# Masking the diagonal blocks in the search for the maxima: from TensorE products to a fused VectorE operation

## The chip, the cores and the metric

The kernel runs on one core of one Trainium2 chip. The metric is the device time of one execution in microseconds; lower is better. All times here are of that core.

## The reference

Two layers, each an attention and a feed-forward, on one sequence of 2048 tokens of 256 features. Both attentions have 16 heads of 16 features and are causal. Cut to what matters (layer 1; layer 0 differs in how q, k and v come about):

```python
scores = jnp.einsum('bhqd,bhkd->bhqk', q, k) / math.sqrt(Hd)
causal = jnp.triu(jnp.full((S, S), -jnp.inf, dtype=scores.dtype), k=1)
scores = scores + causal[None, None]
attn = jax.nn.softmax(scores, axis=-1)
out = jnp.einsum('bhqk,bhkd->bhqd', attn, v)
...
x = x + _layernorm(_L1_attn_ref(_layernorm(x, axis=-1), ...), axis=-1)
x = x + _layernorm(_L1_ffn_ref(_layernorm(x, axis=-1), ...), axis=-1)
```

The softmax needs the largest unmasked score of each row, and the kernel finds it ahead of the exponentials.

## The kernel before, in words

The 2048 tokens are four chunks c of 512 (four tiles t of 128 rows). The 16 heads are four groups g of four: inside a group, e (0 or 1) says in which half of the partitions a head lies, 64 rows each, and i (0 or 1) which of two slots. A *unit* is a chunk and a group (c, g); the order of a layer's 16 units is (0,0), (0,1), the twelve of c = 1, 2, 3, and then (0,2), (0,3). An attention layer does two things for each unit:

- **The search for the maxima** (`maxima`, line 698). Scores are formed with queries on the partitions, a bank of PSUM (128 x 512) at a time, and VectorE reduces each stretch of a row to its largest (line 737), into `pm`. Keys of earlier chunks are unmasked: 16 blocks of 512 for each earlier chunk. The diagonal chunk has for each i and e the blocks "a" (tile 3, 512 keys), "b" (tile 2, 384 keys, and tile 0, 128 keys) and "c" (tile 1, 256 keys). In the last 128 keys of each the causal mask must act. TensorE adds it: two products of 64 rows in bf16 (line 728) put the mask into the bank, and the score products (line 718) of those 128 columns accumulate on top; the other columns are a product of their own. At the end VectorE takes the largest over the chunks and splits it into two parts (lines 758 to 761), and TensorE turns the result (line 770).
- **The weighted sum** (`weighted`, line 785). With keys on the partitions, TensorE forms mask-free scores minus the maximum (lines 802 and 807), ScalarE takes the exponential (line 813), GpSimd zeroes the masked part of diagonal tiles (line 817), and TensorE multiplies by the values (line 824), which accumulate in one bank over all key tiles.

A block of the search uses one half of TensorE's rows, so the blocks of e = 0 and e = 1 run at the same time. The search of unit n may begin once the first score product of unit n-2 is out, and it runs beside the weighted sum of the units before it.

The order in which instructions stand on each engine is written out by a planner (class `Plan`). Each operation is entered with an assumed duration in us, its reads and writes, and a *rank* (its wished place in units). The planner steps through an imagined time: of all operations that are ready it finds the one that could start earliest, and then takes, on that engine, the one of lowest rank among those that could start within `near` of it. `near` is 0.3 us, but 0.1 in the feed-forward stages. Eight PSUM banks are given out by class `Banks`: at most two pairs (for the scores of the weighted sum) and at most four single banks, of which the accumulating value product holds one. The planner fixes only the order; on the chip each engine runs its queue in order and waits on semaphores. Projections of the next chunk, the output projection and the layer norms are entered in the same plan.

Of the kernel before, what the change touches and what calls it, by code (L numbers as in the profile page):

```python
# [11 lines left out]
F32 = mybir.dt.float32  # L12
F32R = mybir.dt.float32r
BF16 = mybir.dt.bfloat16
# [3 lines left out]
ALU = mybir.AluOpType  # L18
AX = mybir.AxisListType
# [11 lines left out]
P = 128  # L31
CH = 512
NCHUNK = T // CH
TPC = CH // P
# [6 lines left out]
NEG = -3.0e38  # L41
# [23 lines left out]
class Buf:  # L65


    def __init__(self, make, ring=None, banks=0):
        self.make, self.ring, self.banks = make, ring, banks
        self.tile, self.at = None, ()  # L70
        self.users, self.writers, self.readers = [], [], []
        if ring is not None and banks != 1:
            ring.asked.append(self)
# [67 lines left out]
class Plan:  # L141
# [6 lines left out]
    free, mode = {}, None  # L148
    LAG = {"DVE": 0.08, "ACT": 0.1, "PE": 0.2}

    def __init__(self, near=0.3, waiting=0.1):
        self.ops, self.near, self.waiting = [], near, waiting

    def op(self, engine, us, fn, r=(), w=(), after=(), hold=(), rank=0.0, mode=None, lanes=(0, 1), lag=0.0):
# [94 lines left out]
def kernel(ctx: ExitStack, tc: tile.TileContext, x_in, cols_in, rows_in, wd_in, wuq_in, rot_in,  # L249
                         wk0_in, wv0_in, rep_in, wo0_in, wq1_in, wk1_in, wv1_in, wo1_in, ffn0_in, ffn1_in, out):  # L250
    nc = tc.nc
    PSUM = bass.MemoryType.PSUM

    const = ctx.enter_context(tc.tile_pool(name="const", bufs=1))
# [9 lines left out]
    def new(pool, shape, dtype, tag, name, n):  # L264

        ring = rings.setdefault(tag, Ring(n, True))
        assert len(ring.slots) == n
        return Buf(lambda: pool.tile(shape, dtype, tag=tag, name=name, bufs=n), ring)

    def bank(name):  # L270
        b = Buf(lambda: psum[:, b.at[0], :], banks, 1)
        return b

    def two_banks(name):
        b = Buf(lambda: psum[:, b.at[0]:b.at[0] + 2, :], banks, 2)
        return b
# [28 lines left out]
    plan = Plan()  # L305
# [8 lines left out]
    def setup(engine, us, fn, rank):  # L314

        done = Buf(lambda: None)
        plan.op(engine, us, fn, r=[late], w=[done], rank=rank)
        return done
# [90 lines left out]
    make_identity(nc, ident)  # L409


    half16 = const.tile([P, 2, P], BF16, tag="half16", name="half16")
    mask_qk = const.tile([P, 2, 2, P], BF16, tag="mask", name="mask")

    def make_mask():
        nc.gpsimd.memset(half16, 0.0)
        nc.gpsimd.memset(mask_qk, 0.0)
        for e in range(2):
            at = half16[64 * e:64 * e + 64]
            nc.gpsimd.affine_select(out=at, in_=at, compare_op=ALU.not_equal, fill=1.0, base=0,  # L420
                                    pattern=[[64, 2], [-1, P]], channel_multiplier=1)
            at = mask_qk[64 * e:64 * e + 64]
            nc.gpsimd.affine_select(out=at, in_=at, compare_op=ALU.is_ge, fill=NEG, base=0,
                                    pattern=[[64, 2], [0, 2], [-1, P]], channel_multiplier=1)

    mask_b = setup("POOL", 2.8, make_mask, rank=-3.2)


    sel_f = const.tile([P, 2, P], F32, tag="sel_f", name="sel_f")
# [233 lines left out]
    class Attention:  # L663


        def __init__(self, L, proj):
            self.L, self.proj = L, proj
            self.V = [values.tile([P, TPC, VW], F32, tag=f"V{c}", name=f"V{L}{c}") for c in range(NCHUNK)]
            self.vb = [Buf(lambda: None) for c in range(NCHUNK)]
            self.kb = [[Buf(lambda: None) for g in range(NG)] for c in range(NCHUNK)]  # L670
            self.tiles, self.k, self.q, self.loaded, self.begun, self.scores = {}, {}, {}, set(), {}, {}
            self.before = {c: [] for c in range(NCHUNK)}
# [25 lines left out]
    def maxima(layer, plan, n, qb, first_rank, span):  # L698

        (c, g), L, kb = UNITS[n], layer.L, layer.kb  # L700
        pm, mx_ = Buf(lambda: pms[n % 2], rpm), Buf(lambda: mx[n % 2], rmx)
        full = 4 * (TPC * c + 3)
        step = [0]

        def rank():
            step[0] += 1
            return first_rank + span * step[0] / full

        def block(name, i, e, terms, us, kc, reduces):


            s = bank(f"m{L}{n}{i}{name}{e}")
            b = slice(64 * e, 64 * e + 64)
            rk = rank()

            def fill():
                def part(t, k0, to, width, start, stop):
                    nc.tensor.matmul(s.t[:, to:to + width], qb.t[b, i, t * P:(t + 1) * P],  # L718
                                     layer.K(kc)[b, 2 * g + i, k0:k0 + width], start=start, stop=stop)

                if kc < c:
                    for t, k0, k1, to in terms:
                        part(t, k0, to, k1 - k0, True, True)
                    return

                lo = terms[0][3] + terms[0][2] - terms[0][1] - P
                for x in range(2):
                    nc.tensor.matmul(s.t[:, lo:lo + P * len(terms)].rearrange("p (d k) -> p d k", k=P), half16[b, x, :],  # L728
                                     mask_qk[b, x, 0:len(terms), :], start=x == 0, stop=False)
                for j, (t, k0, k1, to) in enumerate(reversed(terms)):  # L730
                    part(t, k1 - P, to + k1 - k0 - P, P, False, j == len(terms) - 1)
                part(t, k0, to, k1 - k0 - P, True, True)

            plan.op("PE", us, fill, r=[qb, kb[kc][g], mask_b], w=[s], hold=[pm],
                    after=layer.scores.get(n - 2, ()), rank=rk, mode="row", lanes=(e,))
            for red_us, t, p, src in reduces:
                plan.op("DVE", red_us, lambda t=t, p=p, src=src: nc.vector.tensor_reduce(  # L737
                    pm.t[:, t, e, i, p:p + 1], s.t[:, src], AX.X, ALU.max), r=[s], w=[pm], rank=rk)


        for i in range(2):
            for e in range(2):
                block("a", i, e, [(3, 0, CH, 0)], 0.45, c, [(0.6, 3, 0, slice(0, CH))])
            for e in range(2):
                block("b", i, e, [(2, 0, 3 * P, 0), (0, 0, P, 3 * P)], 0.8, c,
                      [(0.47, 2, 0, slice(0, 3 * P)), (0.2, 0, 0, slice(3 * P, CH))])
            for e in range(2):
                block("c", i, e, [(1, 0, 2 * P, 0)], 0.4, c, [(0.34, 1, 0, slice(0, 2 * P))])
        for i in range(2):
            for t in range(TPC):  # L750
                for p in range(c):
                    for e in range(2):
                        block(f"{t}{p}", i, e, [(t, 0, CH, 0)], 0.233, p, [(0.6, t, 1 + p, slice(0, CH))])

        def close():
            m = mx_.t
            best = small.tile([P, TPC, 2, 2], F32, tag="top", name=f"top{L}{n}", bufs=4)
            nc.vector.tensor_reduce(best, pm.t[:, :, :, :, 0:c + 1], AX.X, ALU.max)
            hl = m.rearrange("p t (e r s) -> p t e r s", e=2, s=2)
            nc.vector.tensor_scalar(hl[:, :, :, 0:2, 0].bitcast(F32R), best, -1.0, None, ALU.mult)  # L760
            nc.vector.scalar_tensor_tensor(hl[:, :, :, 0:2, 1], best, -1.0, hl[:, :, :, 0:2, 0],
                                           ALU.mult, ALU.subtract)

        rk = first_rank + span
        plan.op("DVE", 0.6, close, r=[pm, mx_b], w=[mx_], rank=rk)
        s = bank(f"mt{L}{n}")

        def flip():
            for t in range(TPC):
                nc.tensor.transpose(s.t[:, t * P:(t + 1) * P], mx_.t[:, t, :], ident)  # L770

        mrow = new(const, [P, CH], F32R, "mrow", f"mrow{L}{n}", 3)
        plan.op("PE", 0.5, flip, r=[mx_], w=[s], hold=[mrow], rank=rk, mode="full")
        plan.op("ACT", 0.50, lambda: nc.scalar.copy(mrow.t, s.t), r=[s], w=[mrow], rank=rk)
        return mrow
# [149 lines left out]
    def ffn(own, sg_at, su_at, after=()):  # L925

        L, wb = own.L, own.wb
        wg, wu, wdn = own.part(1, 0, 2), own.part(1, 1, 2), own.part(2, 0, 8)
        with tc.tile_pool(name=f"ff{L}", bufs=1) as ff:
            for tag in ("sl", "fu", "fh", "fl", "yT"):  # L930
                rings.pop(tag, None)
            plan = Plan(0.1, 0.1)

            def back(c, halves, rank):

# [30 lines left out]
            for n_, c in enumerate(own.order):  # L966
# [4 lines left out]
                for fc in range(8):  # L971
                    rk = 10 * n_ + fc
                    s = two_banks(f"gu{L}{c}{fc}")
# [67 lines left out]
    def project1(plan, c, rank):  # L1041
# [4 lines left out]
        for n in range(2) if c == 0 else ():  # L1046
            layer1.begin(plan, n, Buf(lambda n=n: ffn0.part(3, 1, 4)[:, 2 * n:2 * n + 2, :]), 43 + n, 1.0)

    ffn(ffn0, C_SG0, C_SU0, [(1, weights1), (0, lambda plan, rank: project1(plan, 0, rank)),
                             (2, lambda plan, rank: project1(plan, 1, rank))])  # L1050
    load_f8(1, ffn1_in)
    layer1.before[3] = [o for qb, _ in layer1.begun.values() for o in qb.readers]
    wo1, wo1_b = w1.tile([P, 2, D], F32, tag="wo1", name="wo1"), Buf(lambda: None)
    plan = Plan()
    plan.op("SP", 0.1, lambda: nc.sync.dma_start(out=wo1, in_=wo1_in), w=[wo1_b], rank=-5.0, lag=4.0)
    attention(layer1, plan, wo1, wo1_b, "bo1", 0.25, prepare(ffn1))
    ffn(ffn1, C_SG1, C_SU1)


# [113 lines left out]
```

## Time and profile before

| what | value |
|---|---|
| time, median of 3 runs | 1359.1 us (1357.12 to 1359.5) |
| the profiled execution: its time | 1358.62 us |
| its span, first to last instruction | 1356.9 us |
| mean granted TensorE clock | 0.964 |
| attention of layer 0, first search done to last weighted sum | 62.8 to 583.0 us |
| attention of layer 1, the same | 728.2 to 1241.5 us |
| reductions of 512, 384, 256, 128 elements: number | 896, 128, 128, 128 |
| products for the search, mask products | 1664, 768 as built |

The profile is of one execution. A row of the costliest groups names the line, the engine, the operation, what it writes and reads with shapes, the number, then busy time and the mean ns of one, then the engine's idle time before such instructions and what ended it. Busy times are unions of records[...]. The ends of TensorE's records are modelled: its busy share overstates what it does. A row of the waits names who waited for whom, the total in us, how often, and the longest.

### The profile page before, as it was taken

The page shows a single profiled execution, that of the slowest core. Times are in us where ns is not written, and L with a number is a line of the kernel's source. Part 1 is how long each engine was busy: PE and PEld are TensorE (multiplying, and loading weights), DVE is VectorE, ACT ScalarE, POOL GpSimd, SP SyncE. Part 2 cuts the span into 40 slices and gives each one's busy share as a digit, 9 for nine tenths or more (in the row PEclk, how much of TensorE's full clock was granted, in tenths as well). Part 3 has the DMA queues.
Part 4 walks back from the last instruction along what each step waited for, and adds up shares of the span by engine and source line. Part 5 has one row for each costly group of instructions (what it writes and reads, how often), then busy time and mean ns, then how long its engine had stood idle before and what let it go on. Part 6 is the DMA issues. An engine that isn't in the chain of part 4 may idle for free.

```text
span 1356.9 us, 23929 instructions
## 1 busy us (share of the span) xinstructions
PE 1268.2 (93%) x9272; PEld 749.4 (55%) x9272; DVE 932.3 (69%) x1970; ACT 797.7 (59%) x1100; POOL 291.9 (22%) x474
## 2 busy tenths in 40 slices
PE   5889999999999999989978999999999999998996
PEld 3555555555455454568756555445555545455785
DVE  3578888788988782445546868967898888345442
ACT  2336555666556768656633555565655766776563
POOL 4021101200020001346521101010000100023664
PEclk8689999999999999889989999999999999998898
DMA  5550500040000000010056050004000000000000
GB/s 162 177 165 17 172 16 17 5 153 17 17 17 17 1 16 17 25 55 1 3 169 187 1 156 21 27 5 152 17 17 17 1 17 17 17 1 1 0 32 32
DMA packets 39219, 66.29 MB, mean 49 GB/s; under 512 B 6595, under 2 KB 11040, under 8 KB 38976
## 3 DMA queue, kind: packets, MB, share of 16 engines
q1 hardware_dynamic: 38768, 64.32, 15.2%
q8 instruction: 73, 1.20, 0.4%
q0 software_dynamic: 48, 0.11, 0.1%
q10 hardware_dynamic: 288, 0.31, 0.1%
q14 instruction: 42, 0.34, 0.1%
HBM read 41.66 MB, written 23.07 MB: 48 GB/s over the span
## 4 chain that ended last, share of the span: by engine, by line
PE 74%; DVE 12%; ACT 5%; POOL 3%; DMA 3%; issue 2%; SPq 1%; POOLq 0%; ACTq 0%; DVEq 0%
PE banks L824 17%; PE banks L718 12%; PE banks L802 12%; DVE pm L737 9%; PE banks L807 9%; PE banks L588 8%; PE banks L977 7%; PE banks L943 4%; ACT pt L813 3%; PE banks L728 2%; PE banks L504 2%; DMA K<-sc_k 1%; PE banks L837 1%; PE banks L770 1%; ACT yn_a L480 1%
## 5 line engine op out<-in xcount | busy, mean ns | idle before, releaser
L737 DVE TENSOR_REDUCE pm<-banks 128x1 f32<-128x512 f32 (+3 forms) x1280 | 688.0, 603 | 169.3 <-PE banks L718 165.2
L813 ACT ACTIVATE pt<-banks 128x1024 f32<-128x1024 f32 (+3 forms) x640 | 547.2, 895 | 314.2 <-PE banks L807 297.6
L718 PE MATMUL banks<-K,Q 64*128 64x512 f32 (+3 forms) x1608 | 310.9, 383 | 12.3 <-DMA Q<-sc_q 9.0
L802 PE MATMUL banks<-mrow,sel 64*128 64x512 f32 (+3 forms) x1280 | 286.7, 413 | 18.1 <-ACT pt L813 6.3
L824 PE MATMUL banks<-pt,V 128*32 128x512 f32 (+3 forms) x2560 | 300.4, 544 | 1.2 <-ACT pt L813 0.7
L817 POOL TENSOR_SCALAR_AFFINE_SELECT pt<-pt 128x256 f32<-128x256 f32 x256 | 103.1, 406 | 751.6 <-ACT pt L813 749.5
L718 PEld LDWEIGHTS banks<-K,Q 64*128 64x128 f32 x1608 | 181.7, 192 | 124.4 <-DVE pm L737 77.5
L807 PE MATMUL banks<-Q,K 64*128 64x512 f32 (+3 forms) x1248 | 250.0, 368 | 0.0
L802 PEld LDWEIGHTS banks<-mrow,sel 64*128 64x128 f32 x1280 | 143.0, 188 | 167.6 <-ACT pt L813 98.9
L807 PEld LDWEIGHTS banks<-Q,K 64*128 64x128 f32 x1248 | 140.4, 189 | 8.5
L977 PE MATMUL banks<-F,F 128*128 128x512 f32 x512 | 132.4, 401 | 7.7 <-DVE fu L986 7.4
L977 PEld LDWEIGHTS banks<-F,F 128*128 128x128 f32 x512 | 96.8, 191 | 29.3 <-DVE fu L986 8.3
L824 PEld LDWEIGHTS banks<-pt,V 128*32 128x32 f32 x2560 | 52.5, 109 | 85.7 <-issue 69.4
L986 DVE SCALAR_TENSOR_TENSOR fu<-banks,cols,sl 128x512 f32<-128x512 f32 x64 | 47.5, 749 | 73.6 <-ACT sl L984 40.0
L989 POOL TENSOR_TENSOR fl<-fu,fh 128x512 fp32r<-128x512 f32 x64 | 81.9, 1289 | 72.8 <-ACT fh L988 72.8
L728 PE MATMUL banks<-mask,half 64*128 64x128 bf16 (+1 forms) x768 | 90.9, 247 | 1.5 <-DMA Q<-sc_q 0.7
L728 PEld LDWEIGHTS <-half 64*128 64x128 bf16 x768 | 40.8, 97 | 52.1 <-issue 49.5
L988 ACT CAST fh<-fu 128x512 fp32r<-128x512 f32 x64 | 39.6, 620 | 35.3 <-DVE fu L986 33.7
L943 PE MATMUL banks<-fl,F 128*128 128x512 f32 x128 | 51.8, 405 | 2.2 <-POOL fl L989 2.2
L943 PE MATMUL banks<-fh,F 128*128 128x512 f32 x128 | 53.0, 414 | 0.0
L984 ACT ACTIVATE sl<-banks,cols 128x512 f32<-128x512 f32 x64 | 43.3, 688 | 12.0 <-PE banks L977 11.5
L530 DVE SCALAR_TENSOR_TENSOR k<-banks,bk,k 128x512 fp32r<-128x512 f32 x16 | 12.0, 751 | 30.1 <-ACT k L528 27.4
(126 smaller groups left out, 945.9 us busy)
## 6 DMA issues: line engine op xcount, KB each, us to landing
K<-sc_k SPq DMA_DIRECT2D x128, 128.0 KB
Q<-sc_q SPq DMA_DIRECT2D x120, 128.0 KB
sc_q<-q SPq DMA_DIRECT2D x48, 256.0 KB
sc_k<-k SPq DMA_DIRECT2D x32, 256.0 KB
x<-in_x_dram SPq DMA_DIRECT2D x4, 512.0 KB
out_dram<-x SPq DMA_DIRECT2D x4, 512.0 KB
f<-in_ffn_dram SPq DMA_DIRECT2D x2, 768.0 KB
rows<-in_rows_dram SPq DMA_DIRECT2D x1, 1024.0 KB
```

The costliest lines, as they stand in the source:

```text
L588: nc.tensor.matmul(s.t[:, at:at + n], a, b, start=start, stop=stop)
L718: nc.tensor.matmul(s.t[:, to:to + width], qb.t[b, i, t * P:(t + 1) * P], layer.K(kc)[b, 2 * g + i, k0:k0 + width], start=start, stop=stop)
L728: nc.tensor.matmul(s.t[:, lo:lo + P * len(terms)].rearrange("p (d k) -> p d k", k=P), half16[b, x, :], mask_qk[b, x, 0:len(terms), :], sta ...
L737: plan.op("DVE", red_us, lambda t=t, p=p, src=src: nc.vector.tensor_reduce(pm.t[:, t, e, i, p:p + 1], s.t[:, src], AX.X, ALU.max), r=[s], ...
L802: nc.tensor.matmul(s.t[:, e, 0:nq], sel[b:b + 64, i, :], mrow.t[b:b + 64, off:CH], start=True, stop=False)
L807: nc.tensor.matmul(s.t[:, e, 0:nq], layer.K(kt // TPC)[b:b + 64, 2 * g + i, k * P:(k + 1) * P], qb.t[b:b + 64, i, off:CH], start=False, st ...
L813: plan.op("ACT", 0.1 + nq / 620, lambda s=s, pt=pt, nq=nq: nc.scalar.activation(pt.t[:, :, 0:nq], s.t[:, :, 0:nq], AF.Exp, scale=scale), r ...
L817: plan.op("POOL", 0.41, lambda pt=pt: nc.gpsimd.affine_select(out=pt.t[:, :, 0:P], in_=pt.t[:, :, 0:P], compare_op=ALU.is_ge, fill=0.0, ba ...
L824: nc.tensor.matmul(av.t[32 * j:32 * j + 32, off:CH], Vs[kt // TPC][:, kt % TPC, DV * h:DV * h + 32], pts[kt, j // 2].t[:, j % 2, 0:nq], st ...
L943: nc.tensor.matmul(dn[dh].t, wdn[:, fc, dh * P:(dh + 1) * P], halves[fc][j].t, start=fc == 0 and j == 0, stop=fc == 7 and j == 1)
L977: nc.tensor.matmul(s.t[:, i, :], w[:, cc, fc * P:(fc + 1) * P], xT[j].t[:, cc, :], start=n == 0, stop=n == 3)
L989: plan.op("POOL", 1.3, lambda fu=fu, fh=fh, fl=fl: nc.gpsimd.tensor_tensor(fl.t, fu.t, fh.t.bitcast(F32), ALU.subtract), r=[fu, fh], w=[fl ...
```

## The change

The mask leaves TensorE. A float32 tile of 128 x 512 (zero, and the mask in its last 128 columns) is made once. A diagonal block is now filled by plain score products, and VectorE's reduction of it becomes `tensor_tensor_reduce`: sum of the bank and the tail of the mask tile, and the largest of the sums, in one call. Its full-size output goes to a scratch tile `unread` (bf16), the largest to `pm`. Reductions of earlier chunks stay as they were. The two "c" blocks (i = 0 and 1) of a half now share one bank, so a unit has 10 diagonal blocks instead of 12. The assumed durations follow: a reduction of k elements, fused or not, counts 0.07 + k/965 us, a diagonal block 0.233 or 0.25 us on TensorE. The default of `near` falls from 0.3 to 0.1 us, which the feed-forward stages had already.

```diff
-    def __init__(self, near=0.3, waiting=0.1):
+    def __init__(self, near=0.1, waiting=0.1):
...
-    half16 = const.tile([P, 2, P], BF16, tag="half16", name="half16")
-    mask_qk = const.tile([P, 2, 2, P], BF16, tag="mask", name="mask")
+    mask_qk = const.tile([P, CH], F32, tag="mask", name="mask")
+    unread = const.tile([P, CH], BF16, tag="unread", name="unread")
...
-    mask_b = setup("POOL", 2.8, make_mask, rank=-3.2)
+        at = mask_qk[:, CH - P:CH]
+        nc.gpsimd.affine_select(out=at, in_=at, compare_op=ALU.is_ge, fill=NEG, base=0, pattern=[[-1, P]], channel_multiplier=1)
+
+    mask_b = setup("POOL", 1.0, make_mask, rank=-3.2)
...
-        full = 4 * (TPC * c + 3)
+        full = 4 * (TPC * c + 2) + 2
...
-                lo = terms[0][3] + terms[0][2] - terms[0][1] - P
-                for x in range(2):
-                    nc.tensor.matmul(s.t[:, lo:lo + P * len(terms)].rearrange("p (d k) -> p d k", k=P), half16[b, x, :],
-                                     mask_qk[b, x, 0:len(terms), :], start=x == 0, stop=False)
-                for j, (t, k0, k1, to) in enumerate(reversed(terms)):
-                    part(t, k1 - P, to + k1 - k0 - P, P, False, j == len(terms) - 1)
-                part(t, k0, to, k1 - k0 - P, True, True)
-
-            plan.op("PE", us, fill, r=[qb, kb[kc][g], mask_b], w=[s], hold=[pm],
-                    after=layer.scores.get(n - 2, ()), rank=rk, mode="row", lanes=(e,))
-            for red_us, t, p, src in reduces:
-                plan.op("DVE", red_us, lambda t=t, p=p, src=src: nc.vector.tensor_reduce(
-                    pm.t[:, t, e, i, p:p + 1], s.t[:, src], AX.X, ALU.max), r=[s], w=[pm], rank=rk)
+                for i, t, k, to in terms:
+                    nc.tensor.matmul(s.t[:, to:to + k], qb.t[b, i, t * P:(t + 1) * P], layer.K(kc)[b, 2 * g + i, 0:k],
+                                     start=True, stop=True)
+
+            plan.op("PE", us, fill, r=[qb, kb[kc][g]], w=[s], hold=[pm],
+                    after=layer.scores.get(n - 2, ()), rank=rk, mode="row", lanes=(e,))
+            for i, t, k, to in terms:
                 if kc < c:
...
+                    def largest(i=i, t=t, k=k, to=to):
+                        nc.vector.tensor_reduce(pm.t[:, t, e, i, 1 + kc:2 + kc], s.t[:, to:to + k], AX.X, ALU.max)
+                else:
+                    def largest(i=i, t=t, k=k, to=to):
+                        nc.vector.tensor_tensor_reduce(unread[:, 0:k], s.t[:, to:to + k], mask_qk[:, CH - k:CH], 1.0, NEG,
+                                                       ALU.add, ALU.max, pm.t[:, t, e, i, 0:1])
+
+                plan.op("DVE", 0.07 + k / 965, largest, r=[s, mask_b], w=[pm], rank=rk)
...
+        for e in range(2):
+            block("c", e, [(0, 1, 2 * P, 0), (1, 1, 2 * P, 2 * P)], 0.25, c)
...
-            plan = Plan(0.1, 0.1)
+            plan = Plan()
```

## The prediction

> **What bounds the kernel now.** I read the page first (busy shares, slices, costliest groups), then the waits, then the busy times in windows cut at the instants where a unit's search for maxima closes, then the timeline of both engines inside one unit.
>
> ```profile
> PE 1268.2 (93%) x9272; PEld 749.4 (55%) x9272; DVE 932.3 (69%) x1970; ACT 797.7 (59%) x1100; POOL 291.9 (22%) x474
> L737 DVE TENSOR_REDUCE pm<-banks 128x1 f32<-128x512 f32 (+3 forms) x1280 | 688.0, 603 | 169.3 <-PE banks L718 165.2
> ...
> L728 PE MATMUL banks<-mask,half 64*128 64x128 bf16 (+1 forms) x768 | 90.9, 247 | 1.5 <-DMA Q<-sc_q 0.7
> ```
>
> TensorE is busy 93% of the span, and the mask products are 90.9 us of that, but they overlap in two halves of the array, so 90.9 is no saving. The search's reductions (L737) are 688.0 of VectorE's 932.3 us. The waits go both ways between the two engines:
>
> ```profile
> DVE pm L737 <- PE banks L718: 165.2, 156, 7.7
> PEld banks L718 <- DVE pm L737: 77.5, 155, 0.8
> ```
>
> The windows below are layer 1: start and units (0,0) to (1,0); (2,0); (3,0); (3,2); the tail with both last c=0 units. Columns: length, PE, PEld, DVE, ACT, POOL busy, clock, DMA.
>
> ```profile
> 728.00:764.00 36.00, 30.13 (x253) 19.29 (x250) 28.07 (x77) 17.81 (x28) 10.85 (x23) 0.91 0.43 123
> 839.00:868.00 29.00, 27.70 (x228) 14.60 (x232) 27.46 (x56) 14.67 (x18) 3.66 (x9) 1.00 0.06 20
> 986.00:1025.00 39.00, 38.18 (x307) 19.50 (x307) 37.04 (x71) 22.22 (x28) 3.20 (x8) 1.00 0.05 15
> 1072.00:1117.00 45.00, 44.60 (x368) 22.99 (x368) 37.74 (x70) 29.61 (x34) 3.20 (x8) 1.00 0.05 13
> 1161.00:1240.00 79.00, 75.20 (x661) 40.14 (x660) 30.53 (x84) 61.73 (x89) 21.99 (x43) 0.96 0.03 8
> ```
>
> So no single engine bounds the attention. (2,0) and (3,0) are VectorE's: 27.46 of 29 and 37.04 of 39, both 95%, which I take as the most it reaches. The c=3 units are TensorE's with VectorE at 84%. The tail is TensorE's, VectorE mostly idle. A saving on TensorE counts in the last two kinds, a cost on VectorE in the first.
>
> **TensorE, removed.** The timeline of one pair of "a" blocks (both halves of the array):
>
> ```profile
> 1116.51 0.30 PE L728 MATMUL banks<-mask,half 64*128 64x128 bf16 x4
> 1116.61 0.54 PE L718 MATMUL banks<-K,Q 64*128 64x128 f32 x4
> 1116.97 0.40 PE L802 MATMUL banks<-mrow,sel 64*128 64x512 f32 x2
> ```
>
> It occupies TensorE from 1116.51 to 1116.97, 0.46 us. The pairs "b" and "c" read in the same way cost 0.67 and 0.37, so each i costs 1.5 and a unit 3.0 us. After: no mask product (768 fewer), 16 products a unit instead of 28. A pair of 512-wide products takes 0.23 (L802 to L807 in that timeline: 0.23 to 0.24); "a" 0.235, "b" 0.25, and "c", now one pair for both i, 0.25: 2 x 0.485 + 0.25 = 1.2. Saved: 1.8 us a unit, 58 us over 32 units if all of it lay on the path.
>
> **VectorE, added.** 512 of the 1280 reductions become a fused sum and largest. In the built order of the changed kernel each is two VectorE instructions, the stream and a read of the accumulator, and 445 of the 512 streams wait for VectorE's own semaphore, because all write one scratch tile, `unread`; 434 of them stand directly behind the preceding read. The planner counts 0.07 + k/965 us, what a plain reduction costs. What the trace shows of spacing:
>
> ```profile
> 196.14 13.30 DVE L737 TENSOR_REDUCE pm<-banks 128x1 f32<-128x512 f32 x22
> 209.48 0.20 DVE L758 TENSOR_REDUCE top<-pm 128x16 f32<-128x48 f32 x1
> 209.72 0.18 DVE L760 TENSOR_SCALAR mx<-top 128x16 fp32r<-128x16 f32 x1
> 209.93 0.18 DVE L761 SCALAR_TENSOR_TENSOR mx<-top,mx 128x16 f32<-128x16 f32 x1
> 210.02 1.94 DVE L737 TENSOR_REDUCE pm<-banks 128x1 f32<-128x512 f32 x4
> ```
>
> Reductions that don't wait for each other follow every 0.60 us though each record is 0.683 long: the next starts 0.083 before the last ends. The three that wait for VectorE's semaphore start some 0.034 after the end of the one before (209.48 + 0.20 to 209.72). Such a wait costs 0.034 + 0.083 = 0.117 us. Nearest durations:
>
> ```profile
> L573 DVE TENSOR_TENSOR V<-banks,rows 128x512 f32<-128x512 f32 x16 | 10.7, 687 | 4.8 <-PE banks L588 4.8
> L986 DVE SCALAR_TENSOR_TENSOR fu<-banks,cols,sl 128x512 f32<-128x512 f32 x64 | 47.5, 749 | 73.6 <-ACT sl L984 40.0 <-PE banks L977 22.0 <-POOL fl L989 10.1
> L1014 DVE COPY bqr<-banks 128x2 f32<-128x2 f32 x1 | 0.1, 144 | 0.0
> ```
>
> A stream of one PSUM and one SBUF operand: 0.69 (L573; no scalar operand from memory, as here). The read: like the shortest row, 0.15. One fused search of 512: 0.69 - 0.083 + 0.15 + 0.034 = 0.79 against 0.60, so +0.19, and the same at other widths. Low bound: a read of 0.06 and no wait behind it, +0.10 or less; below nothing is excluded, since the stream reads as many elements as the reduction did. High bound: a stream like L986 and a read that starts only after the stream's end, +0.31. I take +0.19, nearest to the rows. 16 a unit: **+3.07 us of VectorE a unit** (6.37 becomes 9.44), 98 us in all.
>
> Here the Trainium skill speaks on both sides. "VectorE: DVE Perf Modes", section "The DRAIN you can't avoid", says that a semaphore after each VectorE operation costs nothing over one at the end; by that rule the fused search costs +0.10 for its second instruction, 51 us in all, and the kernel would gain (below). The rows say -0.083 without and +0.034 with the wait, and the row decides. Its rule for authors to keep the count of operations low, not to fuse for speed, speaks against the change: 512 instructions more.
>
> **Other parts.** Making the mask (POOL, planned 1.0 instead of 2.8 us) lies beside the loads of the start, before the first block; nothing or at most 2 us saved. SP issues the same transfers, ACT and POOL the same operations in nearly the same order: 0. VectorE's new wait holds whatever is queued behind it, mainly further searches, and TensorE waits for their banks; that is counted below. The choice among candidates within 0.1 instead of 0.3 us: the order has 760 runs of one array mode against 777, so 17 switches of 0.1 to 0.2 us, 2 to 3 us gained; by the finer mixing I allow 10 us either way and take 0. The feed-forward stages used 0.1 already.
>
> **The sum.** In the built order the 16 diagonal searches of a unit stand together, mostly 15 in a row, ahead of the others. Between first and last of them TensorE had 8 to 11 us of work in units (3,1) to (3,3); now it has 4.8 to 7.0 (12 to 24 score products at 0.117, 8 to 12 value products at 0.225, the 16 diagonal ones 1.2, switches). VectorE needs 9.44 there. TensorE can be ahead by the three single banks that the accumulating one leaves, about 1.5 us of searches. So:
> - A c=3 unit takes 44.8 (1072.6 to 1117.5, from the end of one search to the next). Diagonal part 8.7 by the same sum, rest 36.1, where TensorE's products sum to 31.7. After: 9.44 - 1.5 = 7.9, and the rest, now holding 32.6 of products, 36.1 x 32.6/31.7 = 37.1. Sum 45.0: +0.2. I use it for seven balanced units a layer: +1.4.
> - Stretches at VectorE's ceiling: (2,0): (27.46 + 3.07)/0.947 = 32.2, +3.2; (3,0): 40.1/0.95 = 42.2, +3.2; the start: (28.07 + 9.2)/0.95 = 39.2 against 36, +3.2.
> - (1,2), (1,3): VectorE about 20.3 of 22; TensorE's saving can't show: 0.
> - The last two units: TensorE alone, -1.8 each, -3.6.
>
> A layer: 9.6 + 1.4 - 3.6 = +7.4; both: +14.8. The profiled execution took 1358.62 (span 1356.9); its sum is 1373.4, and the median of the runs lies 0.5 above it: **1374 us**, 1.1% slower. A measurement of this kernel can tell about 0.2%, 2.7 us, from no change.
>
> **Rivals.** (1) *The fused search is cheap; faster.* If the read is short and the wait hidden (+0.10), a unit's diagonal part is 6.5 instead of 7.9: the seven units gain 1.2 each, (2,0) and (3,0) lose 1.7 each, the start 0, (1,2) and (1,3) gain 0.5 each, the tail 3.6: -9.6 a layer, **1340**. It decides at about +0.15 a search, where the sums cancel. For it: TensorE's 93% and VectorE's 31% idle; against: the 0.117 of a wait, measured. (2) *The read is held until the stream has ended (+0.31)*: +5.0 a unit; start +9, ceilings +5.3 each, (1,2) and (1,3) +1.4 each, seven units +2.1 each, tail -3.6: +34 a layer, **1427**. (3) *Nothing to measure*: +0.15, or the finer choice gives back 15 us: 1359. That the mask products don't go is excluded: the order has none.
>
> **Numbers.** The forecast's case (1362 to 1400): 0.50. Rival 1: 0.31. Rival 2: 0.12. Rival 3: 0.07. Range 1335 to 1412: it takes in most of rival 1, leaving out its end where all TensorE savings show, and the upper half of rival 2. Faster 0.31, same 0.07, slower 0.62.
>
> **What would show it.** Right: L728's rows gone; the fused search's spacing at 512 near 0.79, accumulator reads beside it; VectorE's busy time up by some 60 to 100 us; waits of L718's successor for VectorE above 77.5 in total; (2,0) and (3,0) each longer by about 3; the tail shorter by about 4. Wrong: a spacing of 0.65 or less, c=3 units at 43 us, and TensorE's waits for VectorE no longer than before.

## The result and the profile after

The changed kernel takes 1400.16 us (median of 4 runs, 1397.67 to 1402.74), the kernel before 1358.11 beside it (1357.03 to 1359.5): ratio 1.0309, 95% interval 1.0286 to 1.0332, slower. The forecast was 1374, range 1335 to 1412: the sign and the range held, but the loss is 42 us where 15 were forecast. The profiled execution took 1399.27 (span 1397.6).

From the page of the changed kernel: engines, then the two kinds of search (busy us, mean ns | idle before).

```profile
PE 1271.1 (91%) x8120; PEld 719.1 (51%) x8120; DVE 971.5 (70%) x2482; ACT 795.4 (57%) x1100; POOL 289.3 (21%) x470
...
L720 DVE TENSOR_REDUCE pm<-banks 128x1 f32<-128x512 f32 x768 | 474.3, 681 | 64.8 <-PE banks L712 63.8
...
L723 DVE CUSTOM_DVE_ANT_0 unread<-banks,mask 128x384 bf16<-128x384 f32 (+3 forms) x512 | 250.6, 490 | 100.0 <-PE banks L712 60.0
...
L723 DVE DVE_READ_ACCUMULATOR2_ANT pm<- 128x1 f32 x512 | 42.2, 82 | 0.0
```

1152 products are gone (9272 to 8120), and TensorE's busy time has not fallen at all. VectorE's rose by 39, less than the 60 to 100 that I named as a sign. The waits (who waits <- for whom: us in all, times, longest):

```profile
DVE pm L720 <- PE banks L712: 63.8, 89, 2.4
DVE unread L723 <- PE banks L712: 60.0, 46, 6.3
PEld banks L712 <- DVE pm L720: 56.6, 128, 1.2
PEld banks L712 <- DVE pm L723: 50.0, 91, 1.5
```

TensorE's search now waits 106.6 us for VectorE, 77.5 before; VectorE's 123.8 for TensorE, 165.2 before. VectorE became the later of the two more often. The missing part of its price is in gaps that no busy row shows. VectorE's timeline in unit (2,3) of layer 0 (start, length):

```profile
320.71 0.69 DVE L723 CUSTOM_DVE_ANT_0 unread<-banks,mask 128x512 bf16<-128x512 f32 x1 [0.17 <-DVE pm L723]
321.32 0.08 DVE L723 DVE_READ_ACCUMULATOR2_ANT pm<- 128x1 f32 x1
321.55 0.69 DVE L723 CUSTOM_DVE_ANT_0 unread<-banks,mask 128x512 bf16<-128x512 f32 x1
322.17 0.08 DVE L723 DVE_READ_ACCUMULATOR2_ANT pm<- 128x1 f32 x1
322.39 0.56 DVE L723 CUSTOM_DVE_ANT_0 unread<-banks,mask 128x384 bf16<-128x384 f32 x1
322.88 0.08 DVE L723 DVE_READ_ACCUMULATOR2_ANT pm<- 128x1 f32 x1
323.00 0.29 DVE L723 CUSTOM_DVE_ANT_0 unread<-banks,mask 128x128 bf16<-128x128 f32 x1
```

The read starts 0.08 before its stream ends. In the median over the trace the next operation then starts 0.035 after the read's end where it waits for VectorE's semaphore alone (322.96 to 323.00), and 0.144 where it must wait for TensorE's as well (321.40 to 321.55); VectorE's sequencer executes 241 separate semaphore events for line L723. So 512 to 512 is 0.84 here, and a search of 512 takes 0.77 in the mean of all, longer waits for TensorE left out.

The windows of layer 1 that answer to those of before, cut at the same events (start to (1,0); (2,0); (3,0); (3,2); tail):

```profile
760.00:799.00 39.00, 27.55 (x194) 15.98 (x194) 30.61 (x108) 18.10 (x30) 11.17 (x24) 0.87 0.39 112
872.00:905.00 33.00, 29.85 (x218) 14.19 (x214) 29.36 (x74) 15.95 (x21) 4.07 (x10) 0.95 0.05 17
1023.00:1064.00 41.00, 38.44 (x276) 18.23 (x272) 37.92 (x85) 22.11 (x27) 3.25 (x8) 1.00 0.04 14
1113.00:1158.00 45.00, 43.76 (x327) 20.88 (x323) 38.39 (x84) 30.60 (x35) 3.25 (x8) 1.00 0.05 13
1203.00:1282.00 79.00, 74.81 (x596) 39.74 (x589) 32.05 (x113) 61.98 (x90) 21.69 (x43) 0.96 0.03 8
```

Here the forecast fits but for the tail: 39, 33, 41, 45 and 79 us after 36, 29, 39, 45 and 79. From the first closing of a search to the end of the attention, layer 1 went from 512.8 to 522.0 us, +9.2. Layer 0 went from 519.8 to 546.7, +26.9, after a start that closed its first search 7.0 later; the feed-forward stages, 2.5 shorter together, are no part of it. So the question is layer 0.

One column of the windows was not in the forecast: the granted clock. The records of the clock show only full or half. Before, those at half clock sum to 99.5 us (the last, like that of every trace, runs some 2 us past the span), and in layer 0 there is none between 92 us, in unit (1,0), and the tail. After, they sum to 165 us, 68 of them in layer 0's attention (19 before). Unit (2,3) of layer 0 again, in steps of 3.4 us (length, PE, PEld, DVE, ACT, POOL busy, clock, DMA):

```profile
320.10:323.50 3.40, 3.37 (x29) 2.02 (x28) 2.73 (x13) 1.40 (x2) 0.74 (x2) 1.00 0.03 5
323.50:326.90 3.40, 2.23 (x16) 1.34 (x14) 3.01 (x13) 1.90 (x3) 0.81 (x2) 0.99 0.00 0
326.90:333.70 6.80, 6.80 (x40) 3.40 (x38) 4.65 (x9) 1.37 (x3) 1.22 (x3) 0.50 0.09 26
333.70:337.10 3.40, 3.40 (x33) 2.08 (x29) 3.02 (x5) 3.35 (x5) 0.00 (x0) 1.00 0.33 102
```

From 323.5 to 326.9 VectorE is in its fused searches (3.01 of 3.40 us) and TensorE, waiting for banks, is busy for 2.23. Then its clock is 0.50 for 6.8 us. The Trainium skill ("TensorE: Matmul & The Clock Gate", Part 1) has such a gate, with half clock after an idle window of about 3.4 us. The trace agrees on the length and on 0.50, but here a window with TensorE busy for 66% of it was enough; the nine windows ahead of half clock in the units from (1,1) to (3,3) of both layers had it busy for 45% to 80%.

### The profile page after: what moved, and what is told of

Its sections match the earlier page's. It is cut to its first block, busy times and chain, and to the rows that moved or that the text cites. A ratio compares the mean times of both kernels' runs of the same rounds, so it can differ in the third digit from the quotient of the medians.

```text
span 1397.6 us, 22285 instructions
## 1 busy us (share of the span) xinstructions
PE 1271.1 (91%) x8120; PEld 719.1 (51%) x8120; DVE 971.5 (70%) x2482; ACT 795.4 (57%) x1100; POOL 289.3 (21%) x470
## 3 DMA queue, kind: packets, MB, share of 16 engines
q1 hardware_dynamic: 38768, 64.32, 14.8%
## 4 chain that ended last, share of the span: by engine, by line
PE 61%; DVE 24%; ACT 5%; issue 4%; POOL 2%; DMA 2%; SPq 1%; DVEq 0%; POOLq 0%; ACTq 0%
PE banks L811 14%; DVE unread L723 11%; PE banks L789 10%; DVE pm L720 9%; PE banks L712 9%; PE banks L582 8%; PE banks L964 7%; PE banks L794 6%; PE banks L930 4%; ACT pt L800 3%; PE banks L498 2%; PE banks L824 1%; PE banks L757 1%; SPq L545 1%; DMA K<-sc_k 1%
## 5 line engine op out<-in xcount | busy, mean ns | idle before, releaser
L720 DVE TENSOR_REDUCE pm<-banks 128x1 f32<-128x512 f32 x768 | 474.3, 681 | 64.8 <-PE banks L712 63.8
L712 PE MATMUL banks<-K,Q 64*128 64x512 f32 (+3 forms) x1248 | 299.6, 413 | 29.0 <-DVE pm L723 14.2
L789 PE MATMUL banks<-mrow,sel 64*128 64x512 f32 (+3 forms) x1280 | 293.6, 427 | 31.8 <-DVE pm L723 11.2
L723 DVE CUSTOM_DVE_ANT_0 unread<-banks,mask 128x384 bf16<-128x384 f32 (+3 forms) x512 | 250.6, 490 | 100.0 <-PE banks L712 60.0
L811 PE MATMUL banks<-pt,V 128*32 128x512 f32 (+3 forms) x2560 | 309.1, 557 | 3.9 <-POOL pt L804 3.0
L789 PEld LDWEIGHTS banks<-mrow,sel 64*128 64x128 f32 x1280 | 134.5, 189 | 235.0 <-ACT pt L800 135.7
L712 PEld LDWEIGHTS banks<-K,Q 64*128 64x128 f32 x1248 | 162.2, 192 | 153.9 <-DVE pm L720 56.6
L794 PEld LDWEIGHTS banks<-Q,K 64*128 64x128 f32 x1248 | 133.5, 192 | 7.9
L723 DVE DVE_READ_ACCUMULATOR2_ANT pm<- 128x1 f32 x512 | 42.2, 82 | 0.0
L831 DVE RECIPROCAL r<-banks 128x16 f32<-128x16 f32 x32 | 8.0, 249 | 35.3 <-PE banks L824 35.3
```

What stands on the lines that cost most here:

```text
L712: nc.tensor.matmul(s.t[:, to:to + k], qb.t[b, i, t * P:(t + 1) * P], layer.K(kc)[b, 2 * g + i, 0:k], start=True, stop=True)
L720: nc.vector.tensor_reduce(pm.t[:, t, e, i, 1 + kc:2 + kc], s.t[:, to:to + k], AX.X, ALU.max)
L723: nc.vector.tensor_tensor_reduce(unread[:, 0:k], s.t[:, to:to + k], mask_qk[:, CH - k:CH], 1.0, NEG, ALU.add, ALU.max, pm.t[:, t, e, i, 0:1])
L789: nc.tensor.matmul(s.t[:, e, 0:nq], sel[b:b + 64, i, :], mrow.t[b:b + 64, off:CH], start=True, stop=False)
L794: nc.tensor.matmul(s.t[:, e, 0:nq], layer.K(kt // TPC)[b:b + 64, 2 * g + i, k * P:(k + 1) * P], qb.t[b:b + 64, i, off:CH], start=False, st ...
L811: nc.tensor.matmul(av.t[32 * j:32 * j + 32, off:CH], Vs[kt // TPC][:, kt % TPC, DV * h:DV * h + 32], pts[kt, j // 2].t[:, j % 2, 0:nq], st ...
```

## The experiments

Theory A: the loss is the price of the fused search on VectorE. B: the finer choice (0.1 us) spoils layer 0's order. C: TensorE's gaps behind VectorE halve its clock, and that is the missing part. D: the planner builds on a wrong price. Times are medians, ratios against the kernel before on the same chip.

**e1_near**, in the kernel before:

```
-    def __init__(self, near=0.3, waiting=0.1):
+    def __init__(self, near=0.1, waiting=0.1):
```

> The kernel before with one change: the planner chooses by rank among candidates within 0.1 us of the first instead of 0.3. Theory A (the miss is the price of the fused search on VectorE alone): no difference, 1355 to 1361. Theory B (the finer choice spoils layer 0's order, its start above all): layer 0 longer by 15 to 25 us, 1375 to 1385. Theory C (TensorE's idle gaps behind VectorE halve its clock): as A, with the time at half clock near the 100 us that the trace of before has.

1359.08 us, ratio 1.0005 (0.9991 to 1.0018). With the mask products in place the finer choice does nothing to the total. Its first search also closes late, at 68.5 us for 62.8, and later stages are shorter by about as much: a late start need not show at the end.

**e2_mask**, in the changed kernel: the same line back to 0.3 (the feed-forward stages keep 0.1).

> The changed kernel with the planner's choice put back to 0.3 us: the mask's move alone. A: as the changed kernel, 1396 to 1404. B: about 1372 to 1378, the forecast's +15. C: 1390 to 1402, with 140 to 170 us at half clock as in the changed kernel.

1415.53, ratio 1.0411 (1.0374 to 1.0448). The mask's move alone (with the shared "c" bank and the new assumed durations) loses 58 us, and the finer choice gave back 15 of them. B had the sign wrong, and no theory expected more than 1404. 174 us at half clock.

**e5_plain**, in the changed kernel (here and in the four further kernels built on it, e6, e7b, e10a and e10b, the mask is left out of the search):

```
-                        nc.vector.tensor_tensor_reduce(unread[:, 0:k], s.t[:, to:to + k], mask_qk[:, CH - k:CH], 1.0, NEG,
-                                                       ALU.add, ALU.max, pm.t[:, t, e, i, 0:1])
+                        nc.vector.tensor_reduce(pm.t[:, t, e, i, 0:1], s.t[:, to:to + k], AX.X, ALU.max)
```

> The changed kernel with a plain reduction on the diagonal, so that the mask is left out of the search for the maxima (the weights are still masked): TensorE's saving without VectorE's price. A: VectorE costs what it did, and of 58 us of TensorE about half to all shows: 1310 to 1335. B: 1330 to 1355, layer 0 spoiled as in the changed kernel. C: 1310 to 1335, at 110 us or less of half clock.

1329.78, ratio 0.9783 (0.9753 to 0.9813), 104 us at half clock. Without VectorE's price the removal of the products, with the finer choice, is worth 28 us, and the fused search costs 70. B's forecast is missed too: layer 0's attention takes 510.3 us here, 520.2 before. From its page:

```profile
PE 1225.6 (92%) x8120; PEld 704.1 (53%) x8120; DVE 933.1 (70%) x1970; ACT 794.1 (60%) x1100; POOL 289.3 (22%) x470
```

TensorE's busy time is 45.5 below that of the changed kernel, which issues the same 8120 products in the same order: the difference is waiting inside its records and half clock, not work. The built orders of TensorE, ScalarE, GpSimd and SyncE are the same in the changed kernel, e3, e5, e9 and both e10. That makes these comparable unit by unit.

**e6_plain3**: e5 with the choice at 0.3.

> The plain reduction on the diagonal (the mask left out of the search), with the planner's choice put back to 0.3 us. The mask's move alone gained 15 us by the finer choice, the kernel before none. If the finer choice helps only where VectorE is late: 1326 to 1336. If it suits the order without mask products: 1338 to 1348.

1350.79, ratio 0.9937 (0.9911 to 0.9962). So of the 28 us only 7 to 8 come without the finer choice, and some 20 with it; the time lies above both ranges, nearer to the second: the choice suits the order without mask products, fused search or not. 19 of the 21 us between e6 and e5 are in layer 1, most in units (1,2) (+9.4), (2,1) (+5.3) and (3,1) (+3.3). Why those, I did not settle; 41 us of layer 1 are at half clock in e6 and 17 in e5.

**e3_inplace**, in the changed kernel:

```
-                        nc.vector.tensor_tensor_reduce(unread[:, 0:k], s.t[:, to:to + k], mask_qk[:, CH - k:CH], 1.0, NEG,
+                        nc.vector.tensor_tensor_reduce(s.t[:, to:to + k], s.t[:, to:to + k], mask_qk[:, CH - k:CH], 1.0, NEG,
```

> The changed kernel, the fused search writing its sums over the bank that it reads instead of one shared scratch tile: 10 of a unit's 16 fused searches (all but the second in a bank) no longer wait for VectorE's own semaphore. It takes 0.117 us from those and 0.11 more where the wait was one of two, some 1.7 to 1.9 of the 3.1 to 3.4 us that the searches of a unit cost; the stream itself may be slower with its result in PSUM (not seen yet). A: some half of 1.8 x 32 comes back, 1370 to 1380, the clock no matter. B: 1380 to 1390, layer 0 still longer than layer 1 by the same. C: 1355 to 1370, and the time at half clock falls from 165 to below 125 us.

1367.67, ratio 1.0065 (1.0044 to 1.0086): 32.5 us back. The stream of 512 in the changed kernel (its read takes 82 ns, above), then the stream and the read here:

```profile
L723 DVE CUSTOM_DVE_ANT_0 unread<-banks,mask 128x512 bf16<-128x512 f32 x128 | 88.0, 688 | 44.7 <-PE banks L712 36.4 <-DVE pm L723 0.3
...
L723 DVE CUSTOM_DVE_ANT_0 banks<-banks,mask 128x512 f32<-128x512 f32 x128 | 88.5, 710 | 39.2 <-PE banks L712 35.0 <-PE banks L794 3.9
L723 DVE DVE_READ_ACCUMULATOR2_ANT pm<- 128x1 f32 x512 | 72.8, 142 | 0.0
```

Longer records, and yet faster: where nothing waits behind the read, the next stream starts with it, and 512 to 512 is 0.63. A second instruction alone costs some 0.02 us; the wait is the price. Summed over a unit's 16 diagonal searches (mean distance from each to the next VectorE operation behind it, its read not counted, four of each width, longer waits for other engines left out) a unit costs 6.45 us in e5, 7.94 here, 9.05 in the changed kernel. The price is thus 2.60 us (3.07 forecast), 1.11 of it taken away here; I had said 1.7 to 1.9. The time lands in C's range, just below A's, but half clock is 144 us in this trace, 133 in the mean of the runs, not below 125: neither theory alone.

**e9_alt**: e3, but the second search of a two-search bank writes the scratch tile (`unread[:, 0:k] if to else s.t[:, 0:k]`).

> The kernel that writes sums in place (1367.7), but the second search of a two-search bank writes the scratch tile: it still carries a wait for VectorE's semaphore, now for a write that ended several searches ago. If the price is waiting for the stream just before to drain: spacing behind such a read below 0.06 us, 6 searches a unit lose some 0.17 each, 1340 to 1355. If it is the wait instruction itself: 1364 to 1372.

1361.44, ratio 1.0008 (0.9990 to 1.0027). Behind the read a stream with the wait still starts 0.176 after the read's start, as in e3: the drain theory's sign is not there. The time lies between the two ranges, with a unit at 7.78. The edit tests less than was meant: the second search also reads the bank that the first one wrote in place, and in e3 it waits although its columns are others than the first one's, so here too its wait may be for the search just before it; which write its count names, the trace does not show. Undecided between these.

**e4_cost** and **e8_inpcost**: the planner's price of a fused search, in the changed kernel and in e3.

```
-                plan.op("DVE", 0.07 + k / 965, largest, r=[s, mask_b], w=[pm], rank=rk)
+                plan.op("DVE", (0.07 if kc < c else 0.26) + k / 965, largest, r=[s, mask_b], w=[pm], rank=rk)
```

(0.15 for 0.26 in e8.)

> The changed kernel; only the planner is told a fused search's price, 0.26 + k/965 us instead of 0.07 + k/965. Theory A (the price of the searches): they cost what they cost, 1394 to 1402. Theory D (the plan is built on a wrong price, so TensorE's other work is put too late to fill the wait for VectorE): 1375 to 1390, TensorE's waits for VectorE shorter. Theory C (half clock behind VectorE): follows the time at half clock; if that stays near 165 us, so does the time.

> The kernel that writes the sums in place, with the planner told 0.15 + k/965 for a fused search. A: 1364 to 1370, no difference to 1367.7. D: 1350 to 1362.

1389.15 (ratio 1.0217, 1.0195 to 1.0238) and 1363.40 (1.0036, 1.0005 to 1.0067): in e4 11 us of the 42 come back for the right price, below A's range and at the upper end of D's; in e8 4 us beside e3, between both ranges and no more than either kernel varies from run to run. In e4 layer 0's attention became 22.6 us shorter and layer 1's 6.9 longer; half clock fell in layer 0 from 68 to 41 us and rose in layer 1 from 33 to 55. D is a part at most.

**e7_twice** and its control **e7b_plaintwice**: in the changed kernel and in e5, each diagonal product issued twice.

```
-                for i, t, k, to in terms:
+                for i, t, k, to in terms * (1 if kc < c else 2):
```

> The changed kernel with each diagonal score product issued twice into the same place, at the same planned cost: TensorE does up to 1.2 us more a unit for nothing, inside the stretch in which it waits for VectorE. A: never faster, 1400 to 1430. C: TensorE stays busy enough behind VectorE to keep its clock; the time at half clock falls from 165 to below 130 us and the time to 1380 to 1398 in spite of the work.

> The control of the kernel with doubled products: the plain reduction on the diagonal (the mask left out of the search), products issued twice. Its clock was at half for 104 us, about as before, so C has nothing to give back: A and C both 1335 to 1365, the bare cost of the doubled products over 1329.8.

1414.05 (1.0401, 1.0376 to 1.0427) and 1363.35 (1.0029, 1.0019 to 1.0038). The first is in A's range. The doubled products cost 33.6 us in the control and 14 in the changed kernel, 4.2 in its layer 0 and 9.4 in its layer 1. Half clock fell to 138 us, nearly all of the fall in layer 0's attention (68 to 44). C's forecast of a gain failed; against the control about 10 us of the doubled work are hidden in either layer, though the clock recovered in layer 0 alone. This way of keeping TensorE busy delays the searches and doesn't test the clock cleanly.

**e10a_clump**: e5 with a copy behind each diagonal reduction:

```
                         nc.vector.tensor_reduce(pm.t[:, t, e, i, 0:1], s.t[:, to:to + k], AX.X, ALU.max)
+                        nc.vector.tensor_copy(unread[:, 0:1], pm.t[:, t, e, i, 0:1])
```

> The plain reduction on the diagonal (the mask left out of the search, 1329.8 us), with a one-column copy on VectorE behind each of a unit's 16 diagonal reductions, which waits for it: a dose of some 0.12 to 0.2 us a search, 2 to 3.2 us a unit, without mask tile, scratch writes of 512 or accumulator. If VectorE's time in the clump is the price, whatever spends it, some 0.8 of the dose shows, as for the fused search: 1385 to 1410. If something else of the fused search is (its reads and writes in SBUF, GpSimd held up): below 1365.

1401.62, ratio 1.0318 (1.0288 to 1.0349): +71.8 over e5, as much as the fused search, with no mask tile, no wide write and no accumulator. The distance at 512 is 0.799 (0.604 in e5), the dose 3.0 us a unit. So a dose of VectorE's time is enough to make a loss like that of the fused search, whatever spends it. Per us of dose it is 0.75 here and 0.85 there (70 of 83 us), so up to some 8 of the 70 us may have another cause.

**e10b_spread**: the same copy behind 16 reductions off the diagonal (in c = 0 units, on it).

> The same dose and the same order, but behind 16 of the reductions off the diagonal in every unit with c > 0 (those of chunk 0's keys); the c = 0 units keep it on the diagonal, having no others. The forecast's model (full price only where VectorE is the limit, free beneath TensorE in the rest of a unit): 1345 to 1370. If VectorE's time costs alike wherever it is spent: within 8 us of the kernel with the dose on the diagonal.

1380.68, ratio 1.0160 (1.0130 to 1.0191): +50.9. In the clump the dose costs more, but even spread over stretches that are TensorE's 53% of it shows, above the range that the forecast's idea of cover gave. That idea is too kind, and "costs alike everywhere" is wrong by 21 us.

**The clock, unit by unit.** The changed kernel and e10a have one order and spend nearly the same on VectorE. Units (2,1), (2,2) and (2,3) of layer 0, first in the changed kernel:

```profile
226.20:266.40 40.20, 36.99 (x252) 19.05 (x253) 33.97 (x90) 23.53 (x34) 7.78 (x12) 1.00 0.05 14
266.40:317.00 50.60, 47.51 (x301) 25.52 (x299) 38.24 (x99) 29.81 (x42) 5.73 (x12) 0.97 0.34 105
317.00:352.90 35.90, 34.70 (x246) 17.86 (x244) 28.28 (x67) 22.32 (x27) 3.25 (x8) 0.90 0.05 16
```

and then in e10a:

```profile
225.20:267.60 42.40, 39.10 (x254) 20.68 (x254) 35.33 (x91) 23.61 (x33) 7.76 (x12) 0.92 0.05 13
267.60:321.60 54.00, 50.63 (x301) 26.64 (x298) 39.72 (x98) 29.81 (x42) 5.74 (x12) 0.91 0.32 98
321.60:355.00 33.40, 32.15 (x243) 16.56 (x244) 28.99 (x67) 22.03 (x27) 3.25 (x8) 1.00 0.06 17
```

Of these three units each is longer in the kernel that has the lower clock there. Over the 22 units from (1,1) to (3,3) of both layers and the two tails, the lengths agree within 0.3 us wherever half-clock time agrees, and otherwise differ by 0.34 us per us of half clock (correlation 0.92; two of the seven stretches that differ, (1,1) and the tail of layer 0, have 3.4 us more or less of it and the same length). Repeats of one program say the same: over 87 executions of 13 programs the span rises by 0.24 us per us of half clock (standard error 0.02, from the granted clock of each run). What goes ahead of half clock is plainer. In each of the 14 traces all stretches at half clock begin at one phase of a grid of 3.413 us and last whole steps of it (but for the last). Cut at that grid, the units from (1,1) to (3,3) of all traces have 35 windows at full clock with TensorE busy for less than 70%, and 27 of these are followed by half clock; 20 of 88 are with 70% to 80% busy, and 9 of 3093 with more. Such windows below 80% number 16 in the changed kernel, 19 in e10a, 6 in e10b, 3 in e5 and 1 in the kernel before: VectorE's added time opens them. What they cost is observed, not set by an edit: no run here forced the clock.

## Why the forecast had the sign and missed the size

The sum's own terms against the spans measured, before to after, in us (the start counts from the first instruction in layer 0 and from the first closed search in layer 1; balanced are (1,1), (2,1) to (2,3) and (3,1) to (3,3)):

| term of the sum | forecast, each layer | layer 0 | layer 1 |
|---|---|---|---|
| start, to the close of (1,0) | +3.2 | +5.3 | +3.3 |
| seven balanced units | +1.4 | +15.8 | +0.1 |
| (1,2) and (1,3) | 0 | +4.2 | +0.3 |
| (2,0) and (3,0) | +6.4 | +5.2 | +6.3 |
| tail | -3.6 | +3.5 | -0.8 |
| sum | +7.4 | +34.0 | +9.2 |

The rest of the program is 2.5 shorter. Layer 1 came out near the forecast by terms that cancel; the miss is in layer 0's balanced units and in both tails. e5, which has the saving without the price, parts the two.

**VectorE's price: right.** A search of 512 was to take 0.79 and takes 0.77 in the mean: the read is shorter than I took (0.08), the stream as forecast (0.688), and the wait for two semaphores, which I had not seen in the trace of before, makes up for it. A unit's price is 2.60 us instead of 3.07. The Trainium skill's statement that a semaphore behind each VectorE operation costs nothing extra ("VectorE: DVE Perf Modes", "The DRAIN you can't avoid") would have led to 1340; with 10 of 16 waits gone (e3) the time falls by 32.5, so the rows were the right judge.

**TensorE's saving: about right, by luck.** With no price, my sum gives -16 us a layer: -1.8 for each of seven balanced units and -3.6 in the tail, so -32. Measured, before to e5, it is -28, in the traces -5 in layer 0's attention and -20 in layer 1's, and some 20 of the 28 hang on the finer choice, which I took as nothing. That term was wrong, and in the kernel's favour. In layer 0 e5's balanced units save 1.9 where I had 12.6; 10 us more at half clock in (2,2) are a part of that, and the rest is open.

**What failed is the price's cover.** Without the clock my sum lets 47 of VectorE's 98 us show (+14.8 less -32). Measured (e5 to the changed kernel), 70 of 83 show (2.60 x 32). By the step:
- *Balanced units: +2.0 each for the price.* Right: in the c = 3 units of layer 1 it is +2.4, +1.8 and +1.5, in a regression of all 24 stretches +1.9 where half clock is equal.
- *(1,2), (1,3): 0, and the tail: VectorE mostly idle.* Wrong. From e5 these units pay 1.6 to 3.3 each, the tails 2.4 and 1.2: 12.9 in both layers, about 9 without half clock. With VectorE at 20.3 of 22 us I took it that the saving couldn't show, and left out the cost that had to. The 0 came true in layer 1 by luck: a saving of 3.1 showed there and met a price of 3.4. The tail's saving showed in layer 1 alone (-2.0; +1.1 in layer 0).
- *The start, (2,0) and (3,0): +3.2 each against before.* Right in the mean for (2,0) and (3,0), with 10 us more at half clock in them that the sum did not know. The start of layer 1 took the 39 us that the ceiling rule gave, but by luck: VectorE is busy for 30.61 of them, 78% as before, not 95%.
- *The clock: left out.* I priced TensorE's waiting as waiting only. The stretches from (1,1) to the tail have some 47 us more half clock than in e5; at 0.33 us each, the slope of that pair, it is 15 us, 10 of them in layer 0.

Forecast 14.8, with 9 and 15 added, is 39; the spans differ by 40.7. Terms that cancel are in that sum, so it closes better than its parts are known. The 15 rest on the correlation above, since e7 could not test it.

Of the signs that I named, the spacing, L728's absence, the longer waits and the longer (2,0) and (3,0) came as said; VectorE's busy time (+39 for 60 to 100) did not, because waits leave no busy time, nor did a shorter tail.

**A version that beats both** is e5, 2.2% faster than before. It leaves the mask out of the search: the subtracted value is then a largest over more keys, and the weights are masked after the exponential anyway. Whether it holds for inputs in which a masked score is far above the unmasked ones of its row was not tried. Of those that keep the mask, the best (e1, e8, e9) are level with the kernel before or slightly slower.

## What to carry to other kernels

Where two engines feed each other through a few buffers, cost added to one is covered by the other's surplus less than their busy shares suggest: here 53% to 85% showed, most where it stood in a clump, and units in which VectorE had been busy for 92% paid 1.6 to 3.3 us for 2.6. Ask of every unit of such a sum for both signs, what it saves and what it pays. A scratch tile that nobody reads can be a dear part of an instruction, 32.5 of 70 us here: write what is thrown away to a place that needs no new wait. And where TensorE waits for another engine in a clump, read the granted clock behind it.

## What the hardware showed

- An accumulator read costs some 0.02 us over a plain reduction of 512 if nothing behind it waits, 0.13 with a wait for VectorE's own semaphore and 0.24 if the stream behind it waits for TensorE's as well.
- TensorE need not be idle to lose its clock: windows of 3.4 us with TensorE busy for 45% to 80% of them (its ends are modelled) preceded 3.4 to 13.7 us at 0.50, while 9 of 3093 windows busier than that did. Which unit it hits changes between kernels of one order, so that units of equal work differ by up to 3.5 us.
- A longer record can be the faster instruction: in-place streams and reads (710 and 142 ns for 688 and 82) overlap, and take less of VectorE's time.
